# Deformable sampling: tile pixels re-laid over partitions, half loads on two queues, shifted weight rows

## Chip, cores, metric

One core of a Trainium2 chip. The metric is the device time of one execution in microseconds (us). PE multiplies matrices, DVE, ACT and POOL are the other compute engines, and SP here only issues loads and stores. The kernel before takes 8754 us (median; 8751 to 8761).

## The reference, cut to what matters

Input x is 2 x 256 x 128 x 128, fp32. Layer 0 normalises x and runs three branches (dilations 1, 9 and 12). Each branch computes offsets by a convolution and samples the image at nine shifted places a pixel:

```python
def _deform_dw(x, offset, w, pad, dil):
    ...
    py = yy - pad + ky * dil + off[:, :, 0]
    px = xx - pad + kx * dil + off[:, :, 1]
    sampled = _bilinear(x, py, px)
    return jnp.einsum('bckhw,ck->bchw', sampled, w.reshape(C, K))
```

Layer norm, GELU, a 1x1 convolution and an MLP follow; layer 1 is a 3x3 convolution with ternary weights. The change touches only the sampling.

## The kernel before

Bilinear sampling is written as a matmul. A tile is 16 columns by 8 rows of pixels, so 128 partitions, with 256 channels each (`xs`). The weights `A` are products of two "hat" functions, one in y and one in x, which a front stage has stored in DRAM. PE writes its product to a PSUM tile (`pm`), ACT copies that to `ev`, and DVE adds it into `ring`. The image is walked in row pairs: 2 images x 67 row pairs x 3 branches = 402 units, with 14 tiles to a row pair.

```python
AO = 9; WA = 2 * 12 + W; TR, TC = 8, 16; CI = 10; P = 128
def load_tiles(b, Rt):                       # once per row pair, 14 tiles
    for T in range(NT):
        xt = pool.tile([P, C], F32, name="xs", tag="xs", bufs=20)
        src = bass.AP(..., [[C, TC], [WT * C, TR], [1, C]])    # partition = col * 8 + row
        nc.sync.dma_start(xt, src)
def load_hats(u):                            # 3 ky a unit; hy and hx have 3 buffers each
    for h, start, dims in ((hy, 0, [[0, TC], [3 * HP, TR]]),
                           (hx, 3 * TR * HP, [[3 * HP, TC], [0, TR]])):
        nc.sync.dma_start(h..., bass.AP(hats[b].tensor, base + start, dims + [[1, 3 * HP]]))
def build(u, ky):                            # DVE:  A = hy * hx
    nc.vector.tensor_tensor(dst, hy..., hx..., ALU.mult)
def sample(u, c):                            # c: which half of the channels
    for T in range(0, NT, 2):
        for j in range(2):
            nc.tensor.matmul(pm[:, j, 0:n], lhsT=xts[b, Rt][T + j][:, c*P:(c+1)*P],
                rhs=A[:, m0:m1, AO + (T + j) * CI : AO + (T + j + 1) * CI], ...)
        nc.scalar.copy(ev..., pm...)         # ACT empties the PSUM bank
    ... accumulate(u, c, ev, ky)             # DVE: ring += w * ev
# the norms' rs: four small operations on nc.gpsimd (POOL)
```

Of the 20 xs buffers, 14 are in use, so of the next row pair only six tiles can be loaded ahead. The other eight wait until PE has made its last pass over the old ones. And all loads of the sampling stand in one in-order queue, SP's: a load that waits for PE holds up the hats behind it (SP's xs issues waited 880 us for PE, see below).

Of the kernel before, what the change touches and what calls it, by code (L numbers as in the profile page):

```python
# [19 lines left out]
P = 128  # L20
W = 128
C = 256
# [18 lines left out]
RI, CI = 2, 10  # L41
TR, TC = RI + 2 * REACH, CI + 2 * REACH
NT = -(-(W + 2 * REACH) // CI)
WT = NT * CI + 2 * REACH
AO = 9
WA = 2 * 12 + W
NH = 3 * (TR + TC)
HCH = 108
HALF = 64
# [18 lines left out]
def conv_preact_kernel(ctx: ExitStack, tc: tile.TileContext, t: dict, out: bass.AP):  # L68
    nc = tc.nc
# [45 lines left out]
    def dram(name, shape):  # L115
        return [scratch.tile(shape, F32, name=f"{name}{b}", tag=f"{name}{b}") for b in range(NB)]

    table = dram("table", [HT * WT, C])

    NPAIR = H // RI + 1  # L120
    hats = dram("hats", [NOFF // 6, NPAIR, NH, RI * W])
# [34 lines left out]
    def pair_parity(q):  # L156

        return (REACH + (q % 3 - 1) * DILS[q // 3]) % RI
# [164 lines left out]
    with ExitStack() as actx:  # L323
# [32 lines left out]
        for b in range(NB):  # L356
            stats = ap.tile([P, KC, NGRP, 6], F32, name=f"stats1_{b}", tag=f"stats1_{b}")
            for c in range(KC):
                for g0 in range(0, NGRP, XT):
                    xt = ap.tile([P, XT * NG], F32, name="xt", tag="xt", bufs=3)  # L360
# [258 lines left out]
    def sample_near(pool, psum, k):  # L619
# [3 lines left out]
        HP = RI * W  # L623
# [4 lines left out]
        def load_tiles(b, Rt):  # L628

            xts[b, Rt] = []  # L630
            for T in range(NT):
                xt = pool.tile([P, C], F32, name="xs", tag="xs", bufs=20)
                src = bass.AP(
                    table[b].tensor,
                    table[b].offset + (Rt * RI * WT + T * CI) * C,
                    [[C, TC], [WT * C, TR], [1, C]],
                )
                nc.sync.dma_start(xt, src)
                xts[b, Rt].append(xt)

        def valid(Rt, br, ky):

            s0 = Rt * RI - REACH - ky * DILS[br]
            i0, i1 = max(0, -s0), min(RI, H - s0)
            return (i0, i1) if i0 < i1 else None

        def taps(u):
            return [ky for ky in (-1, 0, 1) if valid(units[u][1], units[u][2], ky)]

        def load_hats(u):  # L650
            b, Rt, br = units[u]
            for ky in taps(u):
                i0, i1 = valid(Rt, br, ky)
                j, i = divmod(
                    Rt * RI - REACH - ky * DILS[br] + i0 + pair_parity(br * 3 + ky + 1), RI
                )
                assert i == i0
                base = hats[b].offset + ((br * 3 + ky + 1) * NPAIR + j) * NH * HP
                hy = pool.tile([P, 3, HP], F32, name="hy", tag="hy", bufs=3)
                hx = pool.tile([P, 3, HP], F32, name="hx", tag="hx", bufs=3)  # L660
                for h, start, dims in (
                    (hy, 0, [[0, TC], [3 * HP, TR]]),
                    (hx, 3 * TR * HP, [[3 * HP, TC], [0, TR]]),
                ):
                    if i1 - i0 == RI:
                        nc.sync.dma_start(
                            h.rearrange("p t n -> p (t n)"),
                            bass.AP(hats[b].tensor, base + start, dims + [[1, 3 * HP]]),
                        )
                    else:  # L670
                        for tap in range(3):
                            nc.sync.dma_start(
                                h[:, tap, i0 * W : i1 * W],
                                bass.AP(
                                    hats[b].tensor,
                                    base + start + tap * HP + i0 * W,
                                    dims + [[1, (i1 - i0) * W]],
                                ),
                            )
                hbs[u, ky] = hy, hx  # L680

        def build(u, ky):
# [8 lines left out]
                Af.tensor,  # L691
                Af.offset + ((ky + 1) * 3 * RI + i0) * WA + AO + REACH - dil,
                [list(Af.ap[0]), [RI * WA + dil, 3], [WA, i1 - i0], [1, W]],
            )
# [51 lines left out]
        def sample(u, c):  # L746
# [13 lines left out]
            for T in range(0, NT, 2):  # L760
# [3 lines left out]
                for j in range(2):  # L764
# [3 lines left out]
                            lhsT=xts[b, Rt][T + j][:, c * P : (c + 1) * P],  # L768
                            rhs=A[:, m0:m1, AO + (T + j) * CI : AO + (T + j + 1) * CI],
                            start=True,  # L770
# [16 lines left out]
        def prepare(u):  # L787

            if u < len(units):
                for ky in taps(u):  # L790
                    build(u, ky)
                if u + 1 < len(units):
                    load_hats(u + 1)

        load_tiles(*units[0][0:2])
        load_hats(0)
        prepare(0)
        prepare(1)
        for u, (b, Rt, br) in enumerate(units):
            if br == BRS[0] and u + len(BRS) < len(units):  # L800
                load_tiles(*units[u + len(BRS)][0:2])
            for c in range(KC):
                sample(u, c)

            while done[b, br] < NGRP and (
                Rt == NR - 1
                or (done[b, br] + 1) * R - 1 < (Rt + 1) * RI - REACH - DILS[br]
            ):
                g = done[b, br]
                r0 = g * R % RINGS[br]  # L810
                ring = k["rings"][br][:, :, r0 : r0 + R, :].rearrange("p k r w -> p k (r w)")
                tail.begin(tail.branch(b, br, g, ring), LAG)
                done[b, br] += 1
# [99 lines left out]
    with cmp.Else():  # L913
        with ExitStack() as bctx:
            psum = bctx.enter_context(tc.tile_pool(name="ps_b", bufs=1, space=PSUM))
            pool = bctx.enter_context(tc.tile_pool(name="bpool", bufs=1))
            k = {
                "A": [pool.tile([P, 9, RI, WA], F32, name=f"A{i}") for i in range(2)],
            }
# [299 lines left out]
```

## Time and profile before

| stage | us | PE busy | DVE busy | DMA share |
|---|---|---|---|---|
| front (norm, offsets, hats) | 0 to 1303 | | | about half |
| sampling | 1303 to 7064 | 5354 of 5761 | 4939 | 0.91 |
| last convolution | 7064 to 8743 | nearly all | | 0.17 |

The lines that the prediction shows are below it. Its lines: first the xs issues (durations ns, min/median/max); then two waits in 1800 to 7000 (us in all, times, longest); then two lines of the timeline (start us, us), the eight xs loads that refill a row pair with the six loaded ahead for the next one, and the first hats load after them:

```profile
L638 SPq DMA_DIRECT2D xs<-table x1876: 514/548/1683, 1287.1 to 7022.6; - x188
SPq L638 <- PE pm L766: 880.3, 1190, 18.0
PE pm L766 <- DMA xs<-table: 0.8, 2, 0.5
3025.13 9.58 SPq L638 DMA_DIRECT2D xs<-table  x14
3034.80 0.55 SPq L666 DMA_DIRECT2D hy<-hats  x1
```

An xs issue holds SP for 0.55 us (median). The refill waits for PE, yet PE has next to no wait for xs: matched from the trace's issues, landings and matmuls, a refilled tile had landed a median of 3.3 us before PE first used it (1.4 us in the tightest tenth).

### The profile page before, as it was taken

The page shows a single profiled execution, that of the slowest core. Times are in us where ns is not written, and L with a number is a line of the kernel's source. Part 1 is how long each engine was busy: PE and PEld are TensorE (multiplying, and loading weights), DVE is VectorE, ACT ScalarE, POOL GpSimd, SP SyncE. Part 2 cuts the span into 40 slices and gives each one's busy share as a digit, 9 for nine tenths or more (in the row PEclk, how much of TensorE's full clock was granted, in tenths as well). Part 3 has the DMA queues.
Part 4 walks back from the last instruction along what each step waited for, and adds up shares of the span by engine and source line. Part 5 has one row for each costly group of instructions (what it writes and reads, how often), then busy time and mean ns, then how long its engine had stood idle before and what let it go on. Part 6 is the DMA issues. An engine that isn't in the chain of part 4 may idle for free. (4 is left out here: it accounts for less than half of the span.)

```text
span 8742.6 us, 125470 instructions
## 1 busy us (share of the span) xinstructions
PE 8006.7 (92%) x41584; PEld 6024.1 (69%) x41584; DVE 5968.9 (68%) x13113; ACT 4523.6 (52%) x9542; POOL 714.5 (8%) x1292
## 2 busy tenths in 40 slices
PE   5977968899999999999989999999999989999999
PEld 3644637788888888887778888888888854444444
DVE  5334436889888898987688988898888844222222
ACT  1332325566666666666656666666666652122121
POOL 0000000011111111111101111111111110000000
PEclk9978968999999999999999999999999989999999
DMA  7445449999999999997798999999999831111111
GB/s 238 138 144 165 140 140 223 240 243 241 241 236 245 241 244 244 244 236 209 194 240 234 242 241 241 241 240 244 234 248 240 229 97 63 56 58 55 56 58 41
DMA packets 994675, 1661.78 MB, mean 190 GB/s; under 512 B 139424, under 2 KB 540112, under 8 KB 989656
## 3 DMA queue, kind: packets, MB, share of 16 engines
q1 hardware_dynamic: 976600, 1620.03, 69.3%
q10 hardware_dynamic: 17408, 33.56, 1.3%
q8 instruction: 333, 5.46, 0.3%
q14 instruction: 334, 2.74, 0.1%
HBM read 1385.08 MB, written 268.09 MB: 189 GB/s over the span
## 5 line engine op out<-in xcount | busy, mean ns | idle before, releaser
L766 PE MATMUL pm<-A,xs 128*128 128x180 f32 (+2 forms) x22288 | 3893.1, 331 | 430.8 <-ACT ev L775 391.8
L766 PEld LDWEIGHTS pm<-A,xs 128*128 128x128 f32 x22288 | 3636.2, 194 | 651.5 <-ACT ev L775 503.6
L775 ACT COPY ev<-pm 128x360 f32<-128x360 f32 (+2 forms) x5572 | 2305.3, 456 | 1572.8 <-PE pm L766 830.9
L740 DVE SCALAR_TENSOR_TENSOR ring<-ev,defw,ring 128x256 f32<-128x256 f32 (+5 forms) x6272 | 2786.8, 463 | 213.6 <-ACT ev L775 44.4
L1078 PE MATMUL pc<-cring,signs 128*128 128x512 bf16 x6912 | 1502.9, 380 | 4.1 <-ACT cring L1059 3.4
L696 DVE TENSOR_TENSOR A<-hy,hx 128x768 f32<-128x768 f32 x1130 | 1020.0, 947 | 372.3 <-DMA hx<-hats 184.0
L1078 PEld LDWEIGHTS <-signs 128*128 128x128 bf16 x6912 | 671.0, 97 | 835.6 <-issue 7.0
L481 ACT ACTIVATE T<-T,rs 128x256 f32<-128x256 f32 x1280 | 663.6, 595 | 3.3 <-POOL rs L477 3.2
L1090 DVE SCALAR_TENSOR_TENSOR o<-pc,wpn,o 128x512 f32<-128x512 f32 x128 | 96.1, 751 | 676.0 <-PE pc L1078 676.0
L474 POOL TENSOR_SCALAR rs<-mv 128x4 f32<-128x4 f32 x320 | 107.4, 336 | 5225.1 <-DVE mv L472 4274.0
L440 PE MATMUL hp<-T,w 128*128 128x512 f32 x1024 | 489.2, 602 | 7.8 <-ACT T L559 7.8
L1086 ACT ACTIVATE o<-xl,l1b 128x512 f32<-128x512 f32 x128 | 92.2, 721 | 739.0 <-DMA out_x<-o 716.2
L207 PE MATMUL pz<-wz,xa 128*128 128x486 f32 x1024 | 465.7, 580 | 6.3 <-DVE zr L214 3.7
L470 DVE BATCH_NORM_STATS2 st<-T 128x6 f32<-128x256 f32 x1280 | 446.9, 412 | 25.3 <-ACT T L462 25.3
L440 PE MATMUL h<-hT,w 128*128 128x512 f32 x1024 | 460.2, 592 | 0.0
L1059 ACT CAST cring<-rest 128x768 bf16<-128x768 f32 (+1 forms) x256 | 211.8, 828 | 461.1 <-PE pc L1078 295.8
L287 ACT ACTIVATE hb<-ph 108x512 f32<-108x512 f32 x384 | 222.4, 598 | 339.0 <-DMA hats<-hb 222.6
L509 ACT ACTIVATE T<-zc,bb,bw 128x512 f32<-128x512 f32 x384 | 278.7, 780 | 229.2 <-PE zc L493 228.5
L493 PEld LDWEIGHTS zc<-ident,T 128*128 128x128 f32 x2560 | 318.0, 148 | 101.1 <-issue 61.8
L493 PE MATMUL zc<-ident,T 128*128 128x128 f32 x2560 | 361.5, 285 | 19.2 <-ACT T L481 13.8
L476 POOL TENSOR_TENSOR rs<-rs,mhalf 128x4 f32<-128x4 f32 x320 | 370.9, 1159 | 0.0
L462 ACT COPY T<-tp 128x512 f32<-128x512 f32 x640 | 346.7, 605 | 30.9 <-PE tp L460 30.3
(107 smaller groups left out, 5388.6 us busy)
## 6 DMA issues: line engine op xcount, KB each, us to landing
hy<-hats SPq DMA_DIRECT2D x1114, 384.0 KB
hx<-hats SPq DMA_DIRECT2D x1114, 384.0 KB
xs<-table SPq DMA_DIRECT2D x1876, 128.0 KB
g12d<-T SPq DMA_DIRECT2D x128, 512.0 KB
other<-g12d SPq DMA_DIRECT2D x128, 512.0 KB
xl<-x1d SPq DMA_DIRECT2D x120, 384.0 KB
hats<-hb SPq DMA_DIRECT2D x256, 144.0 KB
xa<-in_x ACTq DMA_DIRECT2D x64, 512.0 KB
```

Source lines behind the costliest of these rows:

```text
L207: nc.tensor.matmul(pz[:, 0:NZ], lhsT=xt[:, c, r, :], rhs=k["wz"][:, c, :], start=c == 0, stop=c == KC - 1,)
L440: nc.tensor.matmul(out, lhsT=w, rhs=v, start=i == 0, stop=i == n - 1)
L462: nc.scalar.copy(Tv[:, 2 * h : 2 * h + 2, :].rearrange("p j c -> p (j c)"), tp)
L470: pin(nc.vector.bn_stats(st[:, j, :], Tv[:, j, :]))
L476: nc.gpsimd.tensor_tensor(rs[:, 0, :], rs[:, 0, :], mhalf[:, 0:NB4], ALU.pow)
L481: nc.scalar.activation(Tv[:, j, :], Tv[:, j, :], AF.Identity, scale=rs[:, 0, j : j + 1], bias=rs[:, 1, j : j + 1],)
L493: nc.tensor.transpose(zc[:, j * P : (j + 1) * P], Tv[:, j, c * P : (c + 1) * P], ident)
L696: nc.vector.tensor_tensor(dst, hy[:, :, i0 * W : i1 * W].rearrange("p t (i w) -> p t i w", w=W), hx[:, :, i0 * W : i1 * W].rearrange("p t ...
L740: nc.vector.scalar_tensor_tensor(dst, src, w, dst, ALU.mult, ALU.add)
L766: nc.tensor.matmul(pm[:, j, 0:n], lhsT=xts[b, Rt][T + j][:, c * P : (c + 1) * P], rhs=A[:, m0:m1, AO + (T + j) * CI : AO + (T + j + 1) * C ...
L775: nc.scalar.copy(ev[:, m0:m1, T * CI : (T + 2) * CI].rearrange("p m (t j) -> p t m j", j=CI), pm[:, :, 0:n].rearrange("p t (m j) -> p t m ...
L1078: nc.tensor.matmul(pc, lhsT=signs[:, k, ky * 3 + kx, m * P : (m + 1) * P], rhs=xc[:, i, k, ky : ky + R, kx : kx + W], start=j == 0, stop=j ...
```

## The change

The intent: a tile's first four rows go to partitions 0 to 63 and the last four to 64 to 127, so that every load falls into two halves, and those of the hats come from two queues at once. The rows of A move by three floats, because the records of the odd tiles are the slow ones (about 185 ns from start to start, 153 for the even ones).

```diff
-AO = 9
-WA = 2 * 12 + W
+AO = 12
+WA = 28 + W
+TH = TR // 2
@@ load_tiles
-                    [[C, TC], [WT * C, TR], [1, C]],
-                nc.sync.dma_start(xt, src)
+                for half in range(2):
+                    ... offset + ((Rt * RI + half * TH) * WT + T * CI) * C,
+                        [[C, TC], [WT * C, TH], [1, C]],
+                    nc.sync.dma_start(xt[half * P // 2 : (half + 1) * P // 2], src)
@@ load_hats
-                    (hy, 0, [[0, TC], [3 * HP, TR]]),
-                    (hx, 3 * TR * HP, [[3 * HP, TC], [0, TR]]),
-                        nc.sync.dma_start(...)
+                for half, queue in ((0, nc.sync), (1, nc.gpsimd)):
+                        (hy, half * TH * 3 * HP, [[0, TC], [3 * HP, TH]]),
+                        (hx, 3 * TR * HP, [[3 * HP, TC], [0, TH]]),
+                            queue.dma_start(h[ps]..., ...)
```

(The branch for incomplete rows is changed in the same way.)

More of the change, by code (lines that the diff above doesn't have):

```diff
@@ L632, in load_tiles @@
                 xt = pool.tile([P, C], F32, name="xs", tag="xs", bufs=20)
-                src = bass.AP(
-                    table[b].tensor,
-                    table[b].offset + (Rt * RI * WT + T * CI) * C,
-                    [[C, TC], [WT * C, TR], [1, C]],
-                )
-                nc.sync.dma_start(xt, src)
+                for half in range(2):
+                    src = bass.AP(
+                        table[b].tensor,
+                        table[b].offset + ((Rt * RI + half * TH) * WT + T * CI) * C,
+                        [[C, TC], [WT * C, TH], [1, C]],
+                    )
+                    nc.sync.dma_start(xt[half * P // 2 : (half + 1) * P // 2], src)
                 xts[b, Rt].append(xt)
@@ L660, in load_hats @@
                 hx = pool.tile([P, 3, HP], F32, name="hx", tag="hx", bufs=3)
-                for h, start, dims in (
-                    (hy, 0, [[0, TC], [3 * HP, TR]]),
-                    (hx, 3 * TR * HP, [[3 * HP, TC], [0, TR]]),
-                ):
-                    if i1 - i0 == RI:
-                        nc.sync.dma_start(
-                            h.rearrange("p t n -> p (t n)"),
-                            bass.AP(hats[b].tensor, base + start, dims + [[1, 3 * HP]]),
-                        )
-                    else:
-                        for tap in range(3):
-                            nc.sync.dma_start(
-                                h[:, tap, i0 * W : i1 * W],
-                                bass.AP(
-                                    hats[b].tensor,
-                                    base + start + tap * HP + i0 * W,
-                                    dims + [[1, (i1 - i0) * W]],
-                                ),
-                            )
+                for half, queue in ((0, nc.sync), (1, nc.gpsimd)):
+                    ps = slice(half * P // 2, (half + 1) * P // 2)
+                    for h, start, dims in (
+                        (hy, half * TH * 3 * HP, [[0, TC], [3 * HP, TH]]),
+                        (hx, 3 * TR * HP, [[3 * HP, TC], [0, TH]]),
+                    ):
+                        if i1 - i0 == RI:
+                            queue.dma_start(
+                                h[ps].rearrange("p t n -> p (t n)"),
+                                bass.AP(hats[b].tensor, base + start, dims + [[1, 3 * HP]]),
+                            )
+                        else:
+                            for tap in range(3):
+                                queue.dma_start(
+                                    h[ps, tap, i0 * W : i1 * W],
+                                    bass.AP(
+                                        hats[b].tensor,
+                                        base + start + tap * HP + i0 * W,
+                                        dims + [[1, (i1 - i0) * W]],
+                                    ),
+                                )
                 hbs[u, ky] = hy, hx
```

## The prediction

> **What bounds the kernel now.** I first read the busy shares and the 40 slices, to find the stage that the change touches. Then I cut that stage out with busy time by stretch, read the groups of its three engines, and last the waits.
>
> ```profile
> PE 8006.7 (92%) x41584; PEld 6024.1 (69%) x41584; DVE 5968.9 (68%) x13113; ACT 4523.6 (52%) x9542; POOL 714.5 (8%) x1292
> PE   5977968899999999999989999999999989999999
> DVE  5334436889888898987688988898888844222222
> DMA  7445449999999999997798999999999831111111
> ```
>
> The change edits only the deformable sampling (loads of xs, hy, hx, and the layout of A). By tile, the matmuls that read A run from 1303.9 to 7063.9 us: slices 6 to 32, where PE, DVE and DMA are all near nine tenths. The front (0 to 1303) and the last convolution (7064 to the end) contain none of it and must stay. In the sampling stage:
>
> ```profile
> 1303.00:1800.00 497.00, 422.33 (x2469) 393.82 (x2470) 386.79 (x842) 271.36 (x658) 24.86 (x48) 0.92 0.93 233
> 1800.00:7000.00 5200.00, 4872.25 (x26765) 4205.07 (x26766) 4516.73 (x10302) 3478.41 (x7619) 650.44 (x1157) 0.99 0.91 237
> 7000.00:7064.00 64.00, 59.93 (x352) 47.77 (x351) 35.61 (x91) 40.01 (x105) 8.97 (x20) 0.89 0.40 121
> ```
>
> The columns are length, then busy us of PE, weight loads, DVE, ACT, POOL, then granted clock, DMA share and GB/s. In the 5200 us stretch PE is 94% busy, DVE 87%, the 16 DMA engines 91%, ACT 67%, POOL 13%. No engine is alone in front: PE leads, and the other two are so close that little more than a tenth can be won whatever is done to PE.
>
> ```profile
> L766 PE MATMUL pm<-A,xs 128*128 128x180 f32 x19152 | 3481.6, 338 | 335.0 <-ACT ev L775 333.7 <-DMA xs<-table 0.5
> L766 PE MATMUL pm<-A,xs 128*128 128x120 f32 x2688 | 346.6, 286 | 47.6 <-ACT ev L775 47.3 <-DMA xs<-table 0.2
> DVE A L696 <- DMA hx<-hats: 184.0, 125, 13.7
> SPq L666 <- DVE A L696: 1716.7, 419, 15.5
> POOL rs L474 <- DVE mv L472: 3847.8, 240, 54.0
> ```
>
> The first two are PE groups (two MATMUL records make one fp32 product). PE's idle time before them is nearly all for ACT to free a PSUM bank. The others are waits (us in all, times, longest; the DVE one over the whole sampling stage, the two below it over 1800 to 7000): DVE lost only 184 us to hats that had not landed, and the queue that loads them waits for DVE to free the three hats buffers.
>
> Finally I stepped through a run of matmuls in windows of some hundredths of a us; the first column is the start of the earliest one in flight:
>
> ```profile
> 3041.31 0.32 PE L766 MATMUL pm<-A,xs 128*128 128x180 f32 x1
> 3041.46 0.50 PE L766 MATMUL pm<-A,xs 128*128 128x180 f32 x2
> 3041.62 0.53 PE L766 MATMUL pm<-A,xs 128*128 128x180 f32 x2
> 3041.80 0.51 PE L766 MATMUL pm<-A,xs 128*128 128x180 f32 x2
> 3041.99 0.47 PE L766 MATMUL pm<-A,xs 128*128 128x180 f32 x2
> 3042.14 0.50 PE L766 MATMUL pm<-A,xs 128*128 128x180 f32 x2
> 3042.29 0.53 PE L766 MATMUL pm<-A,xs 128*128 128x180 f32 x2
> ```
>
> Starts are 0.15, 0.16, 0.18, 0.19, 0.15, 0.15 us apart: two quick, two slow, in turn. Over all 19,152 records of this shape the gaps between neighbours fall into two heaps, 9,062 of 150 to 160 ns and 8,407 of 180 to 190 ns, centres about 153 and 185. The kernel does tiles in pairs, each tile two records: even tiles are quick, odd tiles slow.
>
> [...] The moving operand is 18 short rows of 10 floats, starting at 9 + 10T in rows of 152 floats. An even T starts at remainder 1 of 4 [...]; an odd T starts at remainder 3 [...]. Those are the slow ones. [...] in 1303 to 7064 a 3072-byte hats packet has a median of 200 ns, though its fastest tenth takes 121 or less, while 2048-byte packets of plain 128-partition loads have 85 ns. [...]
>
> **The change, part by part.** The built programs have the same PE, DVE and ACT order, instruction for instruction; only the memset of A is larger (2808 floats for 2736). What moves is DMA issue: POOL gains about 2,270 rows, SP's row count hardly moves.
>
> *Shifted rows of A.* Offset 12 and pitch 156 make tile starts 12 + 10T: [...] odd tiles should fall from 185 to 153 ns. Half of 19,152 is 9,576 records, times 32 ns is 306 us. The 12-row shapes run at 105 to 125 ns already[...]; 1,344 odd ones at about 10 ns give 13 us. Sum: 320 us off a PE busy time of 5354 us in the stage, 6.0%.
>
> *Does PE's gain reach the end?* In the 5200 us stretch PE idles 328 us and DVE 683 us. The PE gain there is 320 x 5200/5761 = 289 us, leaving 4583 us of work. If PE's idle time stayed, all 289 would be won; but DVE's 4517 us does not shrink, so at 5200 - 289 = 4911 it would be 92% busy, and PE will wait more for banks that ACT can free only after DVE. I let a quarter be lost: 217 us, and with the two short stretches about 240 us.
>
> *DMA.* The packets in 1303 to 7064 add up to 5230 us per engine, 3550 of them hats. Unchanged, they would fill 5230/5520 = 95% of a stage shortened by 240 us; there A's builds would begin to wait. [...] I take 160 to 170 ns after: 284,747 x 34 ns / 16 = 600 us less transfer, share near 83%. That does not shorten the path by itself; it keeps DMA from becoming the bound. The xs halves stay on one queue, [...] so I count no change, only 1,876 more issues: the SP timeline shows 0.52 to 0.60 us each for hats issues, and SP has time.
>
> *POOL.* [...] But the four small rs operations of each normalisation now stand in one line with those issues. From rs done to its ACT use the trace has a median slack of 6.9 us, a lower quarter of 3.7. [...] I charge 30 us.
>
> Sum: 8754 - 240 + 30 = 8544; a little more for shorter hats waits (184 us now, perhaps 20 off): 8525 us.
>
> **The rivals.** *DVE takes over.* It is 87% busy with nothing removed. For: ACT already waits 611 us for DVE's ring operations to free ev. If DVE ran at 97% the stage would be 4939/0.97 = 5092 and the end at 8085; I hold that out of reach, since PE and DVE wait for each other in bursts through two ev buffers. At 89% it would be 5550: 8540. *DMA gets worse.* If SP's half runs ahead of POOL's, [...] packets of 225 ns would add 284,747 x 26 / 16 = 460 us of transfer, a share of 100%, and the time would be 8750 to 8900. Against: both queues are fed from the same DVE release. *POOL in the way.* [...] late rs could eat 100 to 250 us: 8600 to 8750. Against: [...] hats have about a unit to land.
>
> **Range and chances.** 2% is 175 us, so the line lies at 8579. The alignment step is well supported, the DMA one much less. I predict 8525 us, 8380 to 8690 in 8 of 10; faster 0.63, same 0.28, slower 0.09.
>
> **What would show it.** Right: matmul gaps of one heap near 153 ns; the 128x180 group down by about 306 us; hats packets clearly below 199 ns; DVE above 90% busy in the stage; the front and the last convolution within a few us. Wrong: odd tiles still at 185 ns; hats packets above 210 ns with a larger wait of DVE for hats; ACT waiting for rs for hundreds of us; or PE 320 us less busy and the stage as long, its time gone into waits for ev.

## The result, and the profile after

The changed kernel takes **9294 us** (9282 to 9304, 4 runs), against 8754. The ratio is 1.0615, 95% interval 1.0597 to 1.0633: 6% slower. A ratio is the mean time of one kernel's fast runs over that of the other's fast runs of the same rounds, so it is not quite the ratio of the medians quoted.

First the page of the changed kernel: busy shares, and two rows of slices.

```profile
PE 8018.8 (86%) x41584; PEld 5943.0 (64%) x41584; DVE 5992.1 (64%) x13113; ACT 4492.6 (48%) x9542; POOL 1895.1 (20%) x3616
PE   5969947788888888888878888888888888999999
DMA  6455448888888888887688888888888852111111
```

All that was at nine tenths in the sampling stage is now at eight: nothing is saturated, and everything waits for something. The stage now lasts from 1325 to 7614, 6289 us for 5761; the front is 22 us longer and the last convolution as long as before (1679 us).

```profile
1325.00:7614.00 6289.00, 5364.96 (x29585) 4567.02 (x29586) 4960.78 (x11233) 3757.49 (x8380) 1861.59 (x3542) 0.93 0.82 216
L770 PE MATMUL pm<-A,xs 128*128 128x180 f32 x19152 | 3456.4, 336 | 806.0 <-ACT ev L779 458.7 <-DMA xs<-table 340.5 <-ACT T L482 0.6
3053.30 0.32 PE L770 MATMUL pm<-A,xs 128*128 128x180 f32 x1
3053.46 0.62 PE L770 MATMUL pm<-A,xs 128*128 128x180 f32 x3
3053.61 0.62 PE L770 MATMUL pm<-A,xs 128*128 128x180 f32 x3
3053.76 0.62 PE L770 MATMUL pm<-A,xs 128*128 128x180 f32 x3
```

The last four lines step through a run of matmuls as the prediction did. Starts are now 0.15 to 0.16 us apart throughout; over the whole stage 15,748 gaps lie at 150 to 160 ns and hardly any at 180 to 190. **The shift of the rows worked exactly as foreseen.** Yet the group is only 25 us less busy, because the granted clock fell from 0.98 to 0.93 (its records show half speed for 925 us of the stage, against 242 before), and its idle time went from 335 to 806 us. A new name stands among the releasers: xs.

The waits (us in all, times, longest) from 1303 to 7600:

```profile
PE pm L770 <- DMA xs<-table: 350.5, 213, 4.6
DVE A L700 <- DMA hx<-hats: 458.7, 164, 24.1
ACT ev L779 <- DVE ring L744: 804.1, 262, 18.2
```

PE's 0.8 us of waiting for xs has become 350; DVE's wait for hats went from 184 to 459. The queues, by tile, by the timeline and by the issues:

```profile
L640 SPq DMA_DIRECT2D xs<-table x3752: 514/544/1789, 1301.4 to 7582.3; - x198
3014.21 12.86 SPq L640 DMA_DIRECT2D xs<-table  x16
3021.11 0.51 POOL L670 DMA_DIRECT2D hy<-hats  x1 [11.23 <-DMA xs<-table]
3025.70 0.94 PE L770 MATMUL pm<-A,xs 128*128 128x180 f32 x2 [2.62 <-DMA xs<-table]
3027.99 0.51 SPq L670 DMA_DIRECT2D hy<-hats  x1
hy<-hats POOLq DMA_DIRECT2D x1114, 192.0 KB, 5.3
```

An xs issue of 64 KB holds SP as long as one of 128 KB did: 544 against 548 ns. Refilling eight tiles here takes 16 issues and 12.9 us. Over the 132 refills of this form the median is 11.2 us, 9.0 of them inside the issues themselves; before, where the eight stood alone (78 times), it was 5.0 and 4.4. Meanwhile PE stops, twice for over 2 us, for tiles that were issued too late to have landed. The halves do not travel more slowly: from issue to landing an xs load took a median of 3.7 us, against 4.4 before. POOL has issued its half of the next hats at 3021.1; SP's half of the same hats goes out only at 3028.0, because it stands behind the refill.

### The profile page after: what moved, and what is told of

The parts are those of the page before. It is cut to its first block, busy times and chain, and to the rows that moved or that the text cites. A ratio compares the mean times of both kernels' runs of the same rounds, so it can differ in the third digit from the quotient of the medians.

```text
span 9293.4 us, 135227 instructions
## 1 busy us (share of the span) xinstructions
PE 8018.8 (86%) x41584; PEld 5943.0 (64%) x41584; DVE 5992.1 (64%) x13113; ACT 4492.6 (48%) x9542; POOL 1895.1 (20%) x3616
## 5 line engine op out<-in xcount | busy, mean ns | idle before, releaser
L770 PEld LDWEIGHTS pm<-A,xs 128*128 128x128 f32 x22288 | 3562.4, 202 | 1254.9 <-ACT ev L779 694.3
L670 POOL DMA_DIRECT2D hy<-hats x1114 | 595.9, 535 | 2733.3 <-DVE A L700 1901.3
L670 POOL DMA_DIRECT2D hx<-hats x1114 | 590.2, 530 | 42.7 <-issue 35.9
L740 DVE TENSOR_SCALAR ring<-ev,defw 128x256 f32<-128x256 f32 (+1 forms) x788 | 269.4, 343 | 333.6 <-ACT ev L779 333.0
```

The costliest lines, as they stand in the source:

```text
L670: queue.dma_start(h[ps].rearrange("p t n -> p (t n)"), bass.AP(hats[b].tensor, base + start, dims + [[1, 3 * HP]]),)
L770: nc.tensor.matmul(pm[:, j, 0:n], lhsT=xts[b, Rt][T + j][:, c * P : (c + 1) * P], rhs=A[:, m0:m1, AO + (T + j) * CI : AO + (T + j + 1) * C ...
```

## The experiments

Theory 1: the number of DMAs on SP's queue. An xs issue holds SP 0.55 us (median 548 ns at 128 KB, 544 at 64 KB), so cutting each xs load in two makes the refill late, and the hats behind it. Theory 2: half loads get in each other's way and their packets take longer, as the prediction's second rival has it. Theory 3: POOL's queue (late loads, late rs).

**e1_shift_only.** Only the shifted rows, on the kernel before:

```diff
-AO = 9
-WA = 2 * 12 + W
+AO = 12
+WA = 28 + W
```

> The kernel before with the shifted rows of A alone (offset 12, pitch 156), old layout, one queue. All theories agree that this part is a gain: the matmul gaps become one heap near 153 ns, PE loses about 300 us of work, and the time is about 8540 us (8450 to 8650). If it is near 9290, the shift itself is what costs.

8678 us, ratio 0.9922 (0.9905 to 0.9939): a gain, but of 75 us instead of over 200. The stage in one line, first of the kernel before, then of this one:

```profile
1303.00:7064.00 5761.00, 5354.51 (x29584) 4646.65 (x29585) 4939.13 (x11233) 3789.78 (x8380) 684.26 (x1224) 0.98 0.91 235
```

```profile
1303.00:7014.00 5711.00, 5141.87 (x29585) 4452.79 (x29586) 4935.88 (x11233) 3782.38 (x8380) 686.88 (x1224) 0.96 0.90 238
```

Nearly all gaps are at 150 to 160 ns (17,008 of them), worth the 320 us computed. PE's busy time falls by 213 only: the clock records show half speed for 475 us in place of 242 (430 in place of 213 while PE was busy), and half of the 217 more, an estimate of the work lost, is 108 us. Stage less busy time is idle: 406 before, 569 now. So of the 320, some 107 went into a slower clock, 163 into idling, 50 came out in these two traces (75 in the medians).

**e2_no_shift.** The changed kernel with the old rows of A:

```diff
-AO = 12
-WA = 28 + W
+AO = 9
+WA = 2 * 12 + W
```

> The changed kernel with the rows of A put back (offset 9, pitch 152). Every theory in which the new loads, not the shift, cost the time expects no better than the changed kernel: 9300 to 9500 us. If PE no longer sets the pace there at all, the shift is worth nothing and the time is within 1% of 9294.

9465 us, ratio 1.0821. The new loads alone cost 8%; the shift is a gain of some 171 us beside them.

**e3_xs_two_queues.** The changed kernel, second half of each xs tile from POOL:

```diff
-                    nc.sync.dma_start(xt[half * P // 2 : ...], src)
+                    (nc.sync, nc.gpsimd)[half].dma_start(xt[half * P // 2 : ...], src)
```

> The changed kernel with the second half of every xs tile issued from POOL's queue in place of SP's. Theory 1, SP's issue: SP is back at 1876 xs issues of 0.55 us, the waits for xs and for the late first half of the hats go, time 8550 to 8850. Theory 2, [...] the same halves move, so about 9200 to 9350. Theory 3, [...] POOL gets 1876 more, so 9400 or slower.

8740 us, ratio 0.9999 (0.998 to 1.0017). One word takes back 553 of the 616 us between the changed kernel and e1, and the two waits with it:

```profile
DVE A L700 <- DMA hx<-hats: 197.6, 118, 12.0
PE pm L770 <- DMA xs<-table: 5.0, 10, 1.4
```

The layout, the halves and POOL's hats are all still there, and POOL even issues 1,876 more. That is against theory 3. It does not by itself exclude theory 2, since halves from two queues may also get less in each other's way; e4 does.

**e4_twice_issues.** The other way round: the shifted rows in the old layout, SP's queue alone, and each xs tile cut by channels:

```diff
-                nc.sync.dma_start(xt, src)
+                for h0 in range(0, C, C // 2):
+                    src = bass.AP(..., ... + h0, [[C, TC], [WT * C, TR], [1, C // 2]])
+                    nc.sync.dma_start(xt[:, h0 : h0 + C // 2], src)
```

> The kernel before with the shifted rows, and every xs tile loaded by two DMAs of half the channels each (512-byte packets) on SP, in the old layout over all 128 partitions; hats as before on SP alone. Theory 1, SP's issue: SP gets the 1876 more issues, about 1000 us of issue time, and the time is 9000 to 9300. Theories 2 and 3, [...] neither is touched, so the time stays near that of the shifted rows alone, 8550 to 8650.

9267 us, ratio 1.0597, which is 589 us over e1 and within 27 us of the changed kernel, without a half tile and with nothing on POOL. The waits up to 7064 show the same two victims (643 and 171 us over the whole stage):

```profile
DVE A L697 <- DMA hx<-hats: 606.0, 246, 24.7
PE pm L767 <- DMA xs<-table: 154.9, 213, 5.0
```

It is not the transfer: a kilobyte of xs took 60 ns of an engine in e1, and here two packets of 32 ns each. Besides the issue time itself, SP's xs loads waited 682 us up to 7600 for hats and xs loads to land, against 54 in e1 and 377 in the changed kernel: the program lets at most eight loads of this queue be in flight (see e8). Theory 1 predicted both numbers; the others predicted neither.

**e5_hx_pool.** On e1, hx whole from POOL:

```diff
-                        nc.sync.dma_start(
+                        (nc.sync if h is hy else nc.gpsimd).dma_start(
```

> The shifted rows in the old layout, with each hx load issued whole from POOL's queue (hy and xs stay on SP, no halves). It takes about 650 us of issue from SP. If SP's issue still costs something at the old number of issues, 8550 to 8650; if SP had enough room before, 8660 to 8700; if a POOL queue is harmful in itself ([...] late rs), 8720 or slower.

8694 us, ratio 0.9951, no better than e1. At the old number of issues SP has room; taking 1,100 away gains nothing, so the cost that e3 and e4 price sets in only above that number.

**e6_one_queue.** The changed kernel with both hats halves on SP:

```diff
-                for half, queue in ((0, nc.sync), (1, nc.gpsimd)):
+                for half, queue in ((0, nc.sync), (1, nc.sync)):
```

> The changed kernel with both hats halves on SP, so that POOL issues none of them. SP's issue theory: 2228 and some more issues of 0.55 us, over 1200 us, on a queue already late: 9800 to 10400 us. If instead POOL's part were the harm in the changed kernel, it would be faster than 9294.

11265 us, ratio 1.289: the direction of theory 1, and even worse than its number. Now the loads of the norms also come late; ACT waited 1740 us for one of them (xn). POOL's queue was not the harm; it was what kept the changed kernel from this.

**e7_xs_pool.** On e1, xs whole from POOL, hats on SP:

```diff
-                nc.sync.dma_start(xt, src)
+                nc.gpsimd.dma_start(xt, src)
```

> The shifted rows in the old layout, with xs whole on POOL's queue and all hats on SP. The hats no longer stand behind xs loads that wait for PE. If that order was a cost already, 8550 to 8650; if DVE and the banks alone set the pace, 8660 to 8700; if xs waiting at the head of POOL's queue makes the rs operations late, 8720 to 8900.

8917 us, ratio 1.0205 (1.0188 to 1.0223), just above the range of its third case. Now xs stands in front of the norms' rs on POOL (1521 us of waiting for PE there), and ACT waits 256 us for rs, where the changed kernel's ACT waited 8. On POOL's queue too, a load that waits for PE harms what stands behind it.

**e8_hats_pool.** The changed kernel with both hats halves on POOL, xs halves alone on SP:

```diff
-                for half, queue in ((0, nc.sync), (1, nc.gpsimd)):
+                for half, queue in ((0, nc.gpsimd), (1, nc.gpsimd)):
```

> The changed kernel with both hats halves on POOL and both xs halves on SP: SP still issues all 3752 xs halves, but no hats stand behind them. If the harm is hats held up behind xs, 8700 to 8850. If the harm is that xs tiles themselves arrive too slowly at two issues a tile, PE goes on waiting for xs and it stays at 9050 to 9300.

9445 us, ratio 1.0804: above even the upper expectation, a miss. Freeing the hats from standing behind xs does not cure the case; DVE's wait for hats falls to 234 us, but PE's wait for xs rises to 635. The SP queue, in waits up to 7600:

```profile
SPq L640 <- PE pm L770: 2977.0, 887, 25.1
SPq L640 <- DMA xs<-table: 765.0, 872, 2.7
```

SP is now mostly idle, yet it waited 765 us for earlier xs loads of its own. In the built program every DMA of this queue waits for one of eight semaphores in turn, so at most eight are in flight, and in the traces of the kernel before and of the changed one no more than eight were ever between issue and landing; if each is half as large, half as many bytes are. An xs half took a median of 5.8 us from issue to landing here, against 3.7 in the changed kernel. That this is why xs is late in e8 is argued from these numbers, not shown by a run of its own.

**e15_early and e16_late.** Both are e1 with 804 more issues on SP (six tiles of 14 cut by channels as in e4). They differ only in which six: those whose buffers are free well ahead, or those that wait for PE.

```diff
+                n = C // 2 if T < 6 else C          # e15; e16: T >= 8
```

> The shifted rows in the old layout, with only tiles 0 to 5 of every row pair loaded in two DMAs (804 more issues, on tiles whose buffers are free well ahead). If the harm is the number of issues on SP as such, 804/1876 of 589 us: about 8930. If it is the late refill of the eight tiles that wait for PE, small: 8690 to 8780.

> The same with only tiles 8 to 13 in two DMAs (again 804 more issues, on the tiles whose buffers PE frees at the last moment). By the number of issues, about 8930 as well; by the late refill, most of the loss: 8980 to 9200.

e15: 8714 us, ratio 0.9970 (0.9947 to 0.9994). e16: 8857 us, ratio 1.0133 (1.0108 to 1.0158). Against e1's 0.9922, the same 804 issues cost 0.5% in one place and 2.1% in the other. So it is less the number of issues than where they stand: in the refill. e15 and e16, DVE's waits:

```profile
DVE A L698 <- DMA hx<-hats: 185.3, 113, 20.6
```

```profile
DVE A L698 <- DMA hx<-hats: 385.9, 160, 17.6
```

In e16 the victim is the hats behind the refill; PE waited only 67 us for xs itself. e16 came below what I had expected of it: six late tiles do not bring most of what 14 do; on these points the loss grows faster than the number.

**e12_light and e13_light_shift.** Where did the gain of the shift go? The kernel before, and e1, with a third of DVE's accumulation left out (wrong results):

```diff
-            for kx in (0, -1, 1):
+            for kx in (0, -1):
```

> The kernel before with the third column of taps left out of DVE's accumulation (a wrong result on purpose): about 2350 of DVE's ring operations of 0.46 us go, some 1090 us of its 4939 in the sampling stage; PE and the DMA have the same work. If PE was what bound the stage, with DVE only jostling it, 8450 to 8600; if DMA or the three hats buffers bind, 8680 to 8750.

> The same lightened kernel with the shifted rows. If DVE is what swallowed PE's gain (320 us off PE brought only 75), now most of it comes through: 250 to 320 us less than the lightened kernel without the shift. If the transfers of the hats swallowed it, again under 120 us.

8442 us (0.9658), just under the expected range, and 8273 us (0.9459). Taking work from DVE, which was not the busiest engine, made the kernel 3.4% faster; with it gone the shift is worth 169 us, not 75, though not the 250 expected. The stage in e12, then in e13:

```profile
1303.00:6766.00 5463.00, 5287.25 (x29574) 4611.40 (x29574) 3908.86 (x8881) 3809.58 (x8377) 651.00 (x1224) 0.98 0.95 248
```

```profile
1303.00:6601.00 5298.00, 5003.36 (x29565) 4316.44 (x29564) 3904.56 (x8880) 3761.55 (x8376) 654.78 (x1224) 0.98 0.96 256
```

PE is 97% busy in e12. In e13 PE's busy time falls by 284 and the stage by 165; the DMA share is at 0.96. So DVE had swallowed part of the gain and the DMA engines stood behind it; the latter is read from the share, no run took it away.

Not run, because neither built: xs with 28 buffers, meant to take away the wait for PE, and two tiles in one xs load. The fastest correct kernel is e1, the shift alone, 8678 us: faster than both.

## Why the prediction was wrong

By its own steps:

- *Shifted rows*: right. 185 ns became 153 and the PE program lost the work foreseen. Even tiles started at remainder 1 of 4 floats and odd ones at 3; now they start at 0 and 2. The difference of about 32 ns a record of 18 rows is what was measured; why a start at 3 is slow was not shown, and as the pitch of the rows changed with their start, no run separates the two.
- *PE's gain reaches the end*: the mechanism was named (PE would wait for banks behind DVE) but sized at a quarter lost. It was three quarters in e1: 163 us of idling and about 107 us of half clock, for which the prediction had no term. What sets the half clock was not shown: from the kernel before to e1 to the changed kernel it rose from 242 to 475 to 925 us of the stage, and PE's time without work from 406 to 569 to 924.
- *DMA*: hats packets were to fall from 199 to 160 to 170 ns. SP's halves took 196 on average and POOL's 375 for twice the size, so 187; but with the shift alone, without halves, they took 196 too. Halves from two queues brought at most a few per cent; the 160 to 170 were the author's estimate, and what they rested on was not shown.
- ***The step that failed***: "so I count no change, only 1,876 more issues: the SP timeline shows 0.52 to 0.60 us each for hats issues, and SP has time." The cost of an issue was right, and on average SP does have time: 3679 us of issuing in a stage of 6289. But the 14 tiles of a row pair are not spread over it. Eight of them can be loaded only between PE's last use of the old tile in their buffer and its first use of the new one, which before the change were a median of 8.0 us apart. Eight issues, from the first to the last landing, took a median of 8.2 us and kept up, as the tiles are freed one after another; sixteen take 14.1 us and do not, and the hats wait behind. e4 prices the doubling at 589 us, e3 gets 553 back.
- *POOL*: 30 us were charged, the author's estimate; ACT's wait for rs in the changed kernel is 8 us in all. An issue of hats on POOL holds it 0.53 us (hy) or 0.52 (hx) in the median. That fear was unfounded, and e3, with POOL's hats and half of xs, is only 63 us behind e1. What makes up those 63 stays open.
- *The rivals*: "DMA gets worse" (8750 to 8900) and "POOL in the way" (8600 to 8750) were too small as well, and their causes are not what the runs show. "DVE takes over" is in part what e12 and e13 show of the lost gain.

The sum, from e1: 8678, plus 553 for the second xs halves on SP, plus 63 for the rest, gives 9294.

How the 553 divide between the issue time, the limit of eight in flight and the order of the queue was not separated by a run. In the refills themselves about three quarters of the added time is issue time (from 4.4 to 9.0 us, of 5.0 to 11.2). e15 and e16 show that the refill is the place, and e8 that the order alone is not all of it.

## What to carry to other kernels

Count DMAs as instructions, not only as bytes: a queue issues them one by one, here at 0.55 us for 64 KB as for 128, and a load cut in two pays that twice. Do not compare a queue's issue time with the span; look for the burst that must fit between the moment a buffer is freed and the moment its successor is needed, and for what stands behind it (over e1, e7 lost 239 us and e16 179). When two other engines are at nine tenths, expect only a fraction of what one engine saves (here 75 us of 320).
